# A linear-attention block: the output products of two chunks as seven products of halves

## The chip, the core and the metric

The kernel runs on one core of one Trainium2 chip. The time is the device time of one execution in microseconds (us); before the change it is 1804.88 us, the median of three runs (1803.95 to 1805.63).

The core has engines that each run their own queue of instructions in order and meet only at semaphores: TensorE (PE in the profile; PEld is its weight load), VectorE (DVE), ScalarE (ACT), GpSimd (POOL) and SyncE (SP), which here issues nearly all DMAs. Matrix products land in PSUM banks, the rest lies in SBUF.

## The reference, cut to what matters

x has shape 4 x 2048 x 512, all in float32.

```python
x = x + attention(layernorm(x))
x = x + ffn(layernorm(x))

# attention, with its own second norm of the normalized x, gain ln_g and offset ln_b:
qkv  = x_norm @ W_qkv + b_qkv                      # 512 -> 3 * 512
gate = sigmoid(x @ W_gate + b_gate); gate = gate / (mean(gate) + EPS)
q, k = relu(q * gate) ** 2 + EPS, relu(k * gate) ** 2 + EPS    # 16 heads of 32
out_t = (q_t . sum_{s<=t} k_s v_s) / (q_t . sum_{s<=t} k_s + EPS)
return out @ W_proj + b_proj                       # 512 -> 512: the "output product"

# ffn: 512 -> 128 -> 2048, gelu, 2048 -> 128 -> 512
```

## The kernel before, in words

The 8192 rows of x are 64 chunks of 128 tokens, 16 chunks to a sequence. After a start written out by hand for chunks 0 to 3, a loop over c = 4, 6, ..., 62 (line 1065) does one "double step" in each turn: gates, values, queries and keys of chunks c and c + 1; attention of chunk e = c - 1 and then of chunk c; and the feed-forward part of chunks c - 4 and c - 3. A tail finishes chunk 63 and the last feed-forward blocks.

Nothing is reordered by a scheduler: the program is built under a manual schedule (line 879), so each engine executes its instructions in the order of the Python calls. Tiles come from rings of buffers; a write into a buffer waits until the last reader of its former tile has finished. The rings that matter here are `tmp` (5 buffers of 128 x 512), `xn` (2, the normalized inputs), `xp` (12, the chunks of x), `oT` (1, the attention result with features first), `combos` (1) and the PSUM ring `bank` (6).

The gate/value and the query/key products are already done for two chunks at once by a scheme of seven half products (Strassen's, in Winograd's form): `combinations` (407) makes four sums and differences of the two chunks' features on GpSimd, `difference` (940) makes once four sums and differences of the quarters of the weights, and `half_product` (418) does two matmuls over half of the features. The output product is not: `project_out` (729) does four matmuls, 128 x 512 wide, for each chunk, and its `residual` adds the result to x and takes the mean and variance (`moments`, 221).

In one double step the calls in the loop give these orders:

- TensorE: gates and values of the pair (`ps_g`, `ps_gu`, ...), scores of e (`ps_a`), queries and keys (`ps_q` to `ps_k`), the feed-forward's first product (`ps_P`), weighted values of e (`ps_n`, `ps_m`, `ps_S`), four hidden products (`ps_h`, each followed two later by its `ps_Q`), the output product of e (`ps_p`), four more hidden products, scores of c, four more, weighted values of c, the last hidden products, the output product of c, and the two last feed-forward products (`ps_u`). Then the next turn begins with `ps_g`, whose second product `ps_gu` needs the second of the four combinations of chunks c + 2 and c + 3.
- GpSimd, from the output product of e on: the product of queries and running key sums of c (L598, it waits for VectorE's scan L588), the factors of the second layer norm (`second_norm`, L750 to L258: an inverse root by three Newton steps in small operations), the bias of the output product into x (L917), the bias of the feed-forward into two chunks of x (L760), the combinations for the next turn (L412 to L415) and one column of the next keys (L572), which the next scan on VectorE waits for.
- ScalarE, in the second half: the gelu of each hidden product (L797), the normalized inputs of the feed-forward (L264, they wait for `shift_f` of L258), more gelus, and the normalized chunks of a later pair.

The factors of the first norm (`first_norm_factors`, 335: 19 small GpSimd operations) are computed for four chunks at a time, inside `first_moments` ahead of the output product of e, and so in every other turn; in the turn c = 4 alone they stand behind `second_norm`. Input x is loaded at the head of turn c for chunks c + 6 and c + 7, into the buffers of c - 6 and c - 5. `pump(n)` issues the next n pieces of the feed-forward, of which there are 21 in a turn.

Of the kernel before, what the change touches and what calls it, by code (L numbers as in the profile page):

```python
# [60 lines left out]
def tile_linear_attention_block(  # L61
# [36 lines left out]
    of = out.flatten_outer_dims()  # L98

    const = ctx.enter_context(tc.tile_pool(name="const", bufs=1))  # L100
    xp = ctx.enter_context(tc.tile_pool(name="xp", bufs=12))
    work = ctx.enter_context(tc.tile_pool(name="work", bufs=1))
    psum = ctx.enter_context(tc.tile_pool(name="psum", bufs=1, space=bass.MemoryType.PSUM))

# [2 lines left out]
    def bank(name):  # L107
        return psum.tile([P, 512], F32, tag="bank", bufs=6, name=name)
# [38 lines left out]

    load_x(0)
    bg_one = row(b_gate, "a", 4, "bg_one", nc.scalar)
    bp_one = row(b_proj, "oT", 1, "bp_one", nc.scalar)  # L150
    b2_one = row(b2, "back", 1, "b2_one", nc.scalar)
    b_col = columns(ln_b, NK, "b_col", nc.scalar)
    g_col = columns(ln_g, NK, "g_col", nc.scalar)
# [23 lines left out]
    load_half(wqk, B22, w_qkv, 1, D)  # L177
    for c in range(NJ, 2 * NJ):
        load_x(c)
    wp = const.tile([P, NK, D], F32, tag="wp", name="wp")  # L180
    for g in range(NK):
        halves = w_proj[bass.ts(g, P), :].rearrange("(two p) n -> two p n", two=2)
        for half in range(2):
            at = (half ^ (g % 2)) * (P // 2)
            nc.sync.dma_start(wp[at : at + P // 2, g, :], halves[half])
    b1_col = columns(b1, NF, "b1_col", nc.sync)
    u1_sb, pieces = weights(u1, "u1_sb")
    load(pieces)
# [70 lines left out]
        return rs, shift  # L259

    def normalized(src, norm, j, name):
        t = work.tile([P, D], F32, tag="xn", bufs=2, name=name)
        rs, shift = norm
        nc.scalar.activation(  # L264
            t, src, AF.Identity, scale=rs[:, j : j + 1], bias=shift[:, j : j + 1]
        )
        return t
# [384 lines left out]
        return inv  # L652

    def numerators_over(c, num, inv):
        oT = work.tile([P, NK, P], F32, tag="oT", name=f"oT_{c}")
        for odd in range(2):
            by_parity = "p (two odd) t -> p two odd t"
            nc.vector.tensor_tensor(  # L658
                oT.rearrange(by_parity, odd=2)[:, :, odd],
                num[odd][:, 0 : 2 * P].rearrange("p (two t) -> p two t", t=P),  # L660
                inv.rearrange(by_parity, odd=2)[:, :, odd],
                ALU.mult,
            )
        return oT
# [62 lines left out]
        return oT  # L727

    def project_out(c, oT, mv):
        ps = bank(f"ps_p_{c}")  # L730
        for g in range(NK):
            nc.tensor.matmul(ps, oT[:, g, :], wp[:, g, :], start=(g == 0), stop=(g == NK - 1))  # L732

        def residual():

            xt = x_of[c]
            nc.vector.tensor_add(xt, ps, xt)  # L737
            moments(xt, mv, c % NJ)

        return residual  # L740


    x2T_of = {}
# [1 line left out]
    def second_norm(chunks, mv):  # L745

        at = slice(chunks[0] % NJ, chunks[-1] % NJ + 1)
        name = str(chunks[0])
        v = variances(len(chunks), f"f{name}")
        nc.gpsimd.tensor_scalar_add(v, mv[:, at, 1], EPS)  # L750
        rs = inverse_root_by_steps(v, "rs_f", name)
        norm = normalizer(mv[:, at, 0], rs, f"f{name}", nc.gpsimd)

        def normalize(n, c):
            b, j = divmod(c, NP)
            if b not in x2T_of:
                x2T_of[b] = work.tile([P, NP, NQ, NK, DH], F32, tag="x2T", name=f"x2T_{b}")
            xt = x_of[c]
            x2 = normalized(xt, norm, n, f"x2_{c}")
            nc.gpsimd.tensor_add(xt, xt, b2_row)  # L760
            to = x2T_of[b][:, j]
            if c < NC - 1:
                turned_in_quarters(x2, to, f"x2_{c}")
                return None

            return lambda: nc.scalar.copy(
                to.rearrange("p i k t -> p k i t"),
                features_first(x2, f"ps_x2_{c}").rearrange("p k (i t) -> p k i t", t=DH),
            )

        return [lambda n=n, c=c: normalize(n, c) for n, c in enumerate(chunks)]
# [112 lines left out]
    pairs = {}  # L884
    keys = {}
    combos = {}
    waiting = []

    def combine(c):
        combos[c] = combinations(c)  # L890

    def first_moments(n, factors=True):
        nonlocal mv_first
        if n >= NC:
            return
        if n % NJ == 0:
            mv_first = new_moments(f"mv_{n // NJ}")
        moments(x_of[n], mv_first, n % NJ)
        if n % NJ == NJ - 1 and factors:
            first_norm_factors(range(n + 1 - NJ, n + 1), mv_first)  # L900

    def new_keys_in_step(c):
        kT = new_keys(c)
# [14 lines left out]
        return inverse_denominators(e, keys[e][1])  # L918

    def rest_of_attention(e, scores, inv):  # L920
        return weighted(e, scores, pairs[e][1], pairs[e][0], values.pop(e), inv)

    def project_in_step(e, oT, put_off=False):
        nonlocal mv_second
        if e % NJ == 0:
            mv_second = new_moments(f"mv2_{e // NJ}")
        residual = project_out(e, oT, mv_second)
        if put_off:
            return residual
        residual()  # L930

    def nothing():
        pass

    def normalize_pair(c):
        if c < NC:
# [80 lines left out]
    keys[0] = kT, None  # L1017
    factors = sigmoids((2, 3), (g2, g3))
    values_of(2)
    for n in (8, 9):  # L1020
        load_x(n)
    held = {}

    def sums_of_first():
        sums_and_products(0)

    def scores_of_first():
        held["scores"] = scores_in_step(0)

    def features_and_keys():  # L1030
        for turn in turn_xl:
            turn()
        new_keys_in_step(1)

    second = queries_and_keys(
        2,
# [1 line left out]
        sums_of_first,  # L1038
        factors,
        scores_of_first,  # L1040
        features_and_keys,
    )
    inv = denominators_in_step(0)
    oT = rest_of_attention(0, held["scores"], inv)
    sums_and_products(1)
    scores = scores_in_step(1)
    combine(NJ)
    new_keys_in_step(2)
    inv = denominators_in_step(1)
    values_of(3)  # L1050
    project_in_step(0, oT)
    for to in (T1, T2, T4, T3):
        difference(wgv, to, nc.gpsimd)
    oT = rest_of_attention(1, scores, inv)
    sums_and_products(2)
    scores = scores_in_step(2)
    second()
    transfers_back()
    project_in_step(1, oT)
    inv = denominators_in_step(2)  # L1060
    waiting += second_norm([0, 1], mv_second)
    oT = rest_of_attention(2, scores, inv)


    for c in range(NJ, NC, 2):

        e = c - 1
        for n in (c + 6, c + 7):
            if n < NC:
                load_x(n)  # L1070
        held = {}

        def denominators():
            held["inv"] = denominators_in_step(e)

        later = c == NJ
        if later:
            gates_and_values(c, combos[c], lambda: new_keys_in_step(e))
            sums_and_products(e)
            while waiting:  # L1080
                waiting.pop(0)()
            transfers_back()
            residual = project_in_step(2, oT, put_off=True)
            turn_xl = normalize_pair(c + 2)
        else:
            gates_and_values(c, combos[c], denominators)
        scores = scores_in_step(e)

        def turn_features():
            for turn in turn_xl:  # L1090
                turn()

        if later:
            second = queries_and_keys(
                c, combos.pop(c), factors=residual, later=turn_features
            )
        else:
            second = queries_and_keys(c, combos.pop(c))

        rest += feed_forward((c - 4) // NP)  # L1100
        pump(1)
        if later:
            denominators()
        oT = rest_of_attention(e, scores, held["inv"])
        features_back()
        second()
        for n in range(c + 4 if later else c + 6, c + 8):
            first_moments(n, factors=not later)
        pump(4)
        project_in_step(e, oT)  # L1110
        transfers_back()
        pump(2)
        sums_and_products(c)
        waiting += second_norm([e - 1, e], mv_second)
        if later:
            first_norm_factors(range(c + 4, c + 8), mv_first)
        pump(2)


        scores = scores_in_step(c)  # L1120
        inv = denominators_in_step(c)
        pump(4)
        while waiting:
            waiting.pop(0)()
        transfers_back()
        oT = rest_of_attention(c, scores, inv)
        if c + 2 < NC:
            combine(c + 2)
        pump(6)
        project_in_step(c, oT)  # L1130
        if c + 2 < NC:
            pump(len(rest))
            sums_and_products(c + 1)
        for turn in normalize_pair(c + 4):
            turn()
# [4 lines left out]
    scores = scores_in_step(e)  # L1140
    pump(len(rest))
    sums_and_products(e)
    num = rest_of_attention(e, scores, None)
    waiting += second_norm([e - 1], mv_second)
    rest += feed_forward(NC // NP - 2)
    pump(1)
    inv = denominators_in_step(e)
    pump(3)
    oT = numerators_over(e, num, inv)
    waiting.pop(0)()  # L1150
    transfers_back()
    pump(2)
    project_in_step(e, oT)
    norm = second_norm([e], mv_second)
    pump(7)
    turn = norm[0]()
    pump(5)
    turn()
    pump(len(rest) - NP)
    last = feed_forward(NC // NP - 1)  # L1160
    last.pop(0)()
# [51 lines left out]
```

## Time and profile before

| what | value |
|---|---|
| median of three runs | 1804.88 us (1803.95 to 1805.63) |
| the profiled execution, its own time | 1804.6 us |
| its span on the core | 1802.8 us |
| mean granted TensorE clock | 0.998 of full speed |
| TensorE busy with matmuls | 1787.5 us (99%) |
| VectorE busy | 1248.5 us (69%) |
| GpSimd busy | 761.4 us (42%) |
| ScalarE busy | 659.8 us (37%) |
| DMA traffic | 174.21 MB, 97 GB/s on average |

A line of the page's groups reads: line of the code, engine, operation, output and inputs by the program's names, shape, count, then busy time and the mean length of one in ns, then the idle time of the engine ahead of them and what ended it. A line of the timeline reads: start, length, engine, line, operation; in brackets the idle time just before it and the engine that ended it. A float32 matrix product appears as two passes, so a chunk's output product of four matmuls is `x8`. Passes overlap in the pipeline, so their pace is read from start to start.

### The profile page before, as it was taken

What the parts mean: (1) busy time and instruction counts of PE and PEld (TensorE: products, weight loads), DVE (VectorE), ACT (ScalarE), POOL (GpSimd) and SP (SyncE); (2) the same over time, 40 slices, a digit from 0 to 9 for tenths busy, and PEclk for the clock granted to TensorE, in tenths of its full rate; (3) what the DMA queues carried; (4) which work ended last, traced back from release to release, by engine and by line L of the source; (5) the groups of instructions that cost most, each with busy time, mean ns of one, the idle gap of its engine ahead of it and who ended that gap; (6) DMA issues with size and microseconds to landing.
All of it is one profiled execution on the core that took longest, in us unless ns stands there. A gap on an engine that the chain in (4) does not pass through costs nothing.

```text
span 1802.8 us, 34139 instructions
## 1 busy us (share of the span) xinstructions
PE 1787.5 (99%) x12720; PEld 1059.6 (59%) x12720; DVE 1248.5 (69%) x2394; ACT 659.8 (37%) x1171; POOL 761.4 (42%) x1383
## 2 busy tenths in 40 slices
PE   9999999999999999999999999999999999999998
PEld 4455666555665556665556655566655566555666
DVE  7887766776767667676766676776767666766662
ACT  4333433333333334333333333343333334333333
POOL 3545454343544345442444534444334354343432
PEclk9999999999999999999999999999999999999999
DMA  7233332333323333223233232332332332322221
GB/s 228 77 101 93 112 100 89 93 89 101 113 83 93 98 90 112 97 92 91 89 103 107 86 93 90 101 112 92 93 92 90 105 104 87 92 79 90 91 71 47
DMA packets 286153, 174.21 MB, mean 97 GB/s; under 512 B 134558, under 2 KB 234910, under 8 KB 285860
## 3 DMA queue, kind: packets, MB, share of 16 engines
q1 hardware_dynamic: 284926, 172.03, 30.8%
q8 instruction: 100, 1.64, 0.4%
q14 instruction: 65, 0.53, 0.1%
q10 hardware_dynamic: 1062, 0.01, 0.0%
HBM read 89.94 MB, written 82.05 MB: 95 GB/s over the span
## 4 chain that ended last, share of the span: by engine, by line
PE 95%; DVE 2%; DMA 1%; POOL 1%; issue 1%; ACT 0%; SPq 0%; DVEq 0%; ACTq 0%; POOLq 0%
PE ps_h L795 13%; PE ps_Q L801 13%; PE ps_q L420 12%; PE ps_p L732 12%; PE ps_g L420 11%; PE ps_a L612 4%; PE ps_u L420 3%; PE ps_u L819 3%; PE ps_t L420 3%; PE ps_k L420 3%; PE ps_v L420 3%; PE ps_gt L420 3%; PE ps_gu L420 3%; PE ps_P L780 3%; PE ps_n L695 2%; PE ps_n L684 1%
## 5 line engine op out<-in xcount | busy, mean ns | idle before, releaser
L797 ACT ACTIVATE h<-ps_h,b_col 128x256 f32<-128x256 f32 x512 | 233.7, 470 | 292.4 <-PE ps_h L795 292.1
L795 PE MATMUL ps_h<-pT,v_sb 128*128 128x256 f32 x1024 | 303.6, 388 | 1.8 <-DVE pT L791 1.8
L801 PE MATMUL ps_Q<-h,u_sb 128*128 128x256 f32 x1024 | 298.5, 383 | 0.0
L732 PE MATMUL ps_p<-wp,oT 128*128 128x512 f32 x512 | 230.5, 593 | 0.4 <-DVE oT L658 0.4
L795 PEld LDWEIGHTS ps_h<-pT,v_sb 128*128 128x128 f32 x1024 | 187.0, 190 | 45.2 <-issue 15.3
L801 PEld LDWEIGHTS ps_Q<-h,u_sb 128*128 128x128 f32 x1024 | 189.1, 190 | 40.5 <-ACT h L797 17.4
L598 POOL TENSOR_TENSOR qsum<-qT,sums 128x512 f32<-128x512 f32 x64 | 75.4, 1178 | 322.3 <-DVE sums L588 318.2
L420 PE MATMUL ps_q<-wqk,xlT 128*128 128x512 f32 x372 | 177.9, 601 | 0.0
L737 DVE TENSOR_TENSOR x<-ps_p,x 128x512 f32<-128x512 f32 x64 | 44.2, 691 | 186.8 <-PE ps_p L732 186.8
L622 DVE TENSOR_TENSOR a<-ps_a,causal 128x512 f32<-128x512 f32 x256 | 158.3, 680 | 21.8 <-PE ps_a L612 21.8
L564 POOL TENSOR_SCALAR k<-k 128x512 f32<-128x512 f32 x64 | 95.8, 1496 | 170.9 <-DVE blocks_k L283 170.9
L420 PE MATMUL ps_g<-wgv,xlT 128*128 128x512 f32 x360 | 164.6, 593 | 0.1
L732 PEld LDWEIGHTS ps_p<-wp,oT 128*128 128x128 f32 x512 | 97.0, 190 | 97.0 <-issue 88.5
L517 POOL TENSOR_TENSOR u<-u,t 128x512 f32<-128x512 f32 x32 | 40.7, 1271 | 215.9 <-DVE t L515 215.9
L467 POOL TENSOR_TENSOR v<-gu,g 128x512 f32<-128x512 f32 x30 | 38.2, 1273 | 197.3 <-DVE g L462 197.3
L420 PEld LDWEIGHTS ps_g<-wgv,xlT 128*128 128x128 f32 x360 | 68.2, 190 | 86.2 <-issue 84.4
L420 PEld LDWEIGHTS ps_q<-wqk,xlT 128*128 128x128 f32 x372 | 68.1, 189 | 78.4 <-issue 52.9
L399 ACT ACTIVATE gate<-gate 128x512 f32<-128x512 f32 x64 | 40.3, 629 | 189.5 <-DVE gate L395 189.4
L488 ACT ACTIVATE t<-t,rg 128x512 f32<-128x512 f32 x32 | 23.1, 722 | 214.0 <-DVE t L486 214.0
L588 DVE TENSOR_TENSOR_SCAN sums<-keep,kT 128x516 f32<-128x516 f32 x64 | 79.3, 1240 | 28.9 <-ACT kT L577 19.5
L223 DVE BATCH_NORM_STATS2 st<-x 128x6 f32<-128x512 f32 x128 | 86.6, 677 | 8.9 <-DMA x<-in_L_attn_x_dram 6.7
L492 ACT ACTIVATE k<-u,rg 128x512 f32<-128x512 f32 x64 | 45.7, 714 | 118.4 <-DVE u L486 118.4
(175 smaller groups left out, 3213.8 us busy)
## 6 DMA issues: line engine op xcount, KB each, us to landing
x<-in_L_attn_x_dram SPq DMA_DIRECT2D x64, 256.0 KB
dr_q<-blocks_q SPq DMA_DIRECT2D x64, 256.0 KB
dr_k<-blocks_k SPq DMA_DIRECT2D x64, 256.0 KB
qT<-dr_q SPq DMA_DIRECT2D x256, 64.0 KB
kq<-dr_k SPq DMA_DIRECT2D x256, 64.0 KB
out_dram<-x SPq DMA_DIRECT2D x64, 256.0 KB
dr_x<-blocks_x SPq DMA_DIRECT2D x63, 256.0 KB
x2T<-dr_x SPq DMA_DIRECT2D x252, 64.0 KB
```

Source lines behind the costliest of these rows:

```text
L223: nc.vector.bn_stats(st, src)
L420: nc.tensor.matmul(ps, stationary[:, k, :], w[:, slot, k, :], start=(k == 0 and not more), stop=(k == NH - 1), skip_group_check=True,)
L564: nc.gpsimd.tensor_scalar_add(k, k, EPS)
L588: nc.vector.tensor_tensor_scan(sums.rearrange(flat), keep.rearrange(flat), kT.rearrange(flat), 0.0, ALU.mult, ALU.add,)
L598: nc.gpsimd.tensor_mul(qs.rearrange("p k (i t) -> p k i t", t=DH), qT.rearrange("p i k t -> p k i t"), sums[:, :, 1 : P + 1].rearrange("p ...
L612: nc.tensor.matmul(ps[r][:, bass.ts(g, P)], kT[rows, g, 1 : P + 1], qT[rows, :, g, :], start=True, stop=True,)
L622: nc.vector.tensor_tensor(a, ps[r].rearrange("p (g t) -> p g t", t=P), causal.unsqueeze(1).to_broadcast([P, NK, P]), ALU.mult,)
L732: nc.tensor.matmul(ps, oT[:, g, :], wp[:, g, :], start=(g == 0), stop=(g == NK - 1))
L780: nc.tensor.matmul(ps, u1_sb[:, k, :], x2T[:, :, :, k, :].rearrange("p j i t -> p (j i) t"), start=(k == 0), stop=(k == NK - 1),)
L795: nc.tensor.matmul(ps, v1_sb[:, 0, bass.ts(f, P)], held["p"], start=True, stop=True)
L797: nc.scalar.activation(h, ps, AF.Gelu_apprx_tanh, bias=b1_col[:, f : f + 1])
L801: nc.tensor.matmul(held["q"], u2_sb[:, f, :], held["h"].pop(f), start=(f == 0), stop=(f == NF - 1))
```

## The change

Chunks 0 and 1 keep a product each (`project_out`, now in two column halves because of the new layout of the weights). Every later pair e - 1, e is multiplied together by `project_two_out`: seven half products of two matmuls, 128 x 256 wide, in four half banks, with VectorE adding the pieces into the two chunks of x. `output_combinations` makes the four combinations of the two attention results on GpSimd, in the same ring `combos`. `wp` holds seven quarters and differences in place of the plain weight; it is loaded in 16 DMAs of half the width instead of 8, and its differences are made on GpSimd ahead of the loop.

With it go: `oT` has two buffers; the normalized inputs are drawn from `tmp`, and `xn` is gone; `xp` has 10 buffers, and x is loaded two chunks later; the first norm's factors are computed for two chunks in every turn up to c = 58, behind `second_norm`; the output product of c is gone from the second half of the turn, and the weighted values of c stand behind the last hidden product, just ahead of the two last feed-forward products; in the tail, chunks 62 and 63 are normalized together and both turned on TensorE.

```diff
-    xp = ctx.enter_context(tc.tile_pool(name="xp", bufs=12))
+    xp = ctx.enter_context(tc.tile_pool(name="xp", bufs=10))
...
-    wp = const.tile([P, NK, D], F32, tag="wp", name="wp")
+    wp = const.tile([P, 7, NH, D // 2], F32, tag="wp", name="wp")
...
-            nc.sync.dma_start(wp[at : at + P // 2, g, :], halves[half])
+            for col, slot in enumerate(((B11, B12), (B21, B22))[g // NH]):
+                nc.sync.dma_start(
+                    wp[at : at + P // 2, slot, g % NH, :], halves[half][:, bass.ts(col, D // 2)]
+                )
...
     def normalized(src, norm, j, name):
-        t = work.tile([P, D], F32, tag="xn", bufs=2, name=name)
+        t = temp(name)
...
+    def output_combinations(early, late, name):
+        s = work.tile([P, 4, NH, P], F32, tag="combos", name=f"outs_{name}")
+        lo, hi = slice(0, NH), slice(NH, NK)
+        nc.gpsimd.tensor_add(s[:, 0], early[:, lo], early[:, hi])
+        nc.gpsimd.tensor_sub(s[:, 1], s[:, 0], late[:, lo])
+        nc.gpsimd.tensor_sub(s[:, 2], late[:, lo], early[:, lo])
+        nc.gpsimd.tensor_sub(s[:, 3], late[:, hi], s[:, 1])
+        return s
...
+    def project_two_out(c, early, late, s, mv):
...
+        xe, xl = x_of[c], x_of[c + 1]
+        sums = temp(f"p_{c}")
+        u2, u3 = sums[:, left], sums[:, right]
+        t1 = temp(f"p1_{c}")[:, left]
...
+        ps5 = half_bank("pt")
+        half_product(ps5, s[:, 0], wp, T1)
+        nc.vector.tensor_add(xe[:, right], ps5, xe[:, right])
+        ps1 = half_bank("p")
+        half_product(ps1, late[:, lo], wp, B11)
+        nc.scalar.copy(t1, ps1)
+        ps6 = half_bank("pu")
+        half_product(ps6, s[:, 1], wp, T2)
+        nc.vector.tensor_add(u2, ps6, t1)
+        half_product(ps1, late[:, hi], wp, B21, more=True)
+        nc.vector.tensor_add(xl[:, left], ps1, xl[:, left])
+        ps7 = half_bank("pv")
+        half_product(ps7, s[:, 2], wp, T3)
+        nc.vector.tensor_add(u3, ps7, u2)
+        half_product(ps5, s[:, 3], wp, B22, more=True)
+        nc.vector.tensor_add(xl[:, right], xl[:, right], u2)
+        nc.vector.tensor_add(xl[:, right], ps5, xl[:, right])
+        half_product(ps7, early[:, hi], wp, T4, more=True)
+        moments(xl, mv, (c + 1) % NJ)
+        nc.vector.tensor_add(xe, xe, sums)
+        nc.vector.tensor_add(xe[:, left], ps7, xe[:, left])
+        moments(xe, mv, c % NJ)
...
-    def first_moments(n, factors=True):
+    def first_moments(n):
...
-        if n % NJ == NJ - 1 and factors:
-            first_norm_factors(range(n + 1 - NJ, n + 1), mv_first)
+        if n == 2 * NJ - 1:
+            first_norm_factors(range(NJ, 2 * NJ), mv_first)
...
-    for n in (8, 9):
-        load_x(n)
...
+    for to in (T1, T2, T4, T3):
+        difference(wp, to, nc.gpsimd)
...
     for c in range(NJ, NC, 2):
         e = c - 1
-        for n in (c + 6, c + 7):
+        for n in (c + 4, c + 5):
             if n < NC:
                 load_x(n)
...
-        oT = rest_of_attention(e, scores, held["inv"])
+        rest_of_attention(e, scores, held["inv"])
+        combine_results(e)
         features_back()
         second()
-        for n in range(c + 4 if later else c + 6, c + 8):
-            first_moments(n, factors=not later)
+        for n in (c + 4, c + 5):
+            first_moments(n)
         pump(4)
-        project_in_step(e, oT)
+        project_two_in_step(e)
         transfers_back()
         pump(2)
         sums_and_products(c)
         waiting += second_norm([e - 1, e], mv_second)
-        if later:
-            first_norm_factors(range(c + 4, c + 8), mv_first)
+        if c + 4 < NC:
+            first_norm_factors([c + 4, c + 5], mv_first)
         pump(2)
         scores = scores_in_step(c)
         inv = denominators_in_step(c)
         pump(4)
         while waiting:
             waiting.pop(0)()
         transfers_back()
-        oT = rest_of_attention(c, scores, inv)
         if c + 2 < NC:
             combine(c + 2)
-        pump(6)
-        project_in_step(c, oT)
+        pump(len(rest) - NP)
+        rest_of_attention(c, scores, inv)
         if c + 2 < NC:
             pump(len(rest))
             sums_and_products(c + 1)
```

In the start, the turn of chunks 4 and 5 into features-first form moves ahead of the scores of chunk 0, and `project_in_step(2)` is gone from the turn c = 4.

More of the change, by code (lines that the diff above doesn't have):

```diff
@@ L149, in tile_linear_attention_block @@
     bg_one = row(b_gate, "a", 4, "bg_one", nc.scalar)
-    bp_one = row(b_proj, "oT", 1, "bp_one", nc.scalar)
+    bp_one = row(b_proj, "oT", 2, "bp_one", nc.scalar)
     b2_one = row(b2, "back", 1, "b2_one", nc.scalar)
@@ L654, in numerators_over @@
     def numerators_over(c, num, inv):
-        oT = work.tile([P, NK, P], F32, tag="oT", name=f"oT_{c}")
+        oT = work.tile([P, NK, P], F32, tag="oT", bufs=2, name=f"oT_{c}")
         for odd in range(2):
@@ L730, in project_out @@
         ps = bank(f"ps_p_{c}")
[L731 to L740, printed above, removed]
+        for col, slots in enumerate(((B11, B21), (B12, B22))):
+            for g in range(NK):
+                nc.tensor.matmul(
+                    ps[:, bass.ts(col, D // 2)],
+                    oT[:, g, :],
+                    wp[:, slots[g // NH], g % NH, :],
+                    start=(g == 0),
+                    stop=(g == NK - 1),
+                    skip_group_check=True,
+                )
@@ new lines, in project_out @@
+        xt = x_of[c]
+        nc.vector.tensor_add(xt, ps, xt)
+        moments(xt, mv, c % NJ)
+    def output_combinations(early, late, name):
[6 more added lines that the diff above has]
+        return s
@@ new lines, in project_two_out, with half_bank @@
+    def project_two_out(c, early, late, s, mv):
+        lo, hi = slice(0, NH), slice(NH, NK)
+        left, right = slice(0, D // 2), slice(D // 2, D)
+        xe, xl = x_of[c], x_of[c + 1]
+        sums = temp(f"p_{c}")
+        u2, u3 = sums[:, left], sums[:, right]
+        t1 = temp(f"p1_{c}")[:, left]
+        def half_bank(name):
+            return bank(f"ps_{name}_{c}")[:, left]
+        ps5 = half_bank("pt")
[20 more added lines that the diff above has]
+        moments(xe, mv, c % NJ)
@@ L761, in normalize @@
             to = x2T_of[b][:, j]
-            if c < NC - 1:
+            if c < NC - 2:
                 turned_in_quarters(x2, to, f"x2_{c}")
@@ L886, in tile_linear_attention_block @@
     combos = {}
+    results = {}
     waiting = []
@@ L920, in rest_of_attention, with project_in_step @@
     def rest_of_attention(e, scores, inv):
-        return weighted(e, scores, pairs[e][1], pairs[e][0], values.pop(e), inv)
-    def project_in_step(e, oT, put_off=False):
+        results[e] = weighted(e, scores, pairs[e][1], pairs[e][0], values.pop(e), inv)
+    def project_in_step(e):
         nonlocal mv_second
@@ L926, in project_in_step, with combine_results, project_two_in_step @@
             mv_second = new_moments(f"mv2_{e // NJ}")
[L927 to L933, printed above, removed]
+        project_out(e, results.pop(e), mv_second)
+    def combine_results(e):
+        combos["out"] = output_combinations(results[e - 1], results[e], e - 1)
+    def project_two_in_step(e):
+        nonlocal mv_second
+        if (e - 1) % NJ == 0:
+            mv_second = new_moments(f"mv2_{e // NJ}")
+        project_two_out(
+            e - 1, results.pop(e - 1), results.pop(e), combos.pop("out"), mv_second
+        )
     def normalize_pair(c):
@@ L1027, in scores_of_first @@
     def scores_of_first():
-        held["scores"] = scores_in_step(0)
-    def features_and_keys():
         for turn in turn_xl:
             turn()
-        new_keys_in_step(1)
+        held["scores"] = scores_in_step(0)
     second = queries_and_keys(
@@ L1040, in tile_linear_attention_block @@
         scores_of_first,
-        features_and_keys,
+        lambda: new_keys_in_step(1),
     )
     inv = denominators_in_step(0)
-    oT = rest_of_attention(0, held["scores"], inv)
+    rest_of_attention(0, held["scores"], inv)
     sums_and_products(1)
@@ L1050, in tile_linear_attention_block @@
     values_of(3)
-    project_in_step(0, oT)
+    project_in_step(0)
     for to in (T1, T2, T4, T3):
         difference(wgv, to, nc.gpsimd)
-    oT = rest_of_attention(1, scores, inv)
+    rest_of_attention(1, scores, inv)
     sums_and_products(2)
@@ L1058, in tile_linear_attention_block @@
     transfers_back()
-    project_in_step(1, oT)
+    project_in_step(1)
+    for to in (T1, T2, T4, T3):
+        difference(wp, to, nc.gpsimd)
     inv = denominators_in_step(2)
     waiting += second_norm([0, 1], mv_second)
-    oT = rest_of_attention(2, scores, inv)
+    rest_of_attention(2, scores, inv)
     for c in range(NJ, NC, 2):
         e = c - 1
-        for n in (c + 6, c + 7):
+        for n in (c + 4, c + 5):
             if n < NC:
@@ L1082, in tile_linear_attention_block @@
             transfers_back()
-            residual = project_in_step(2, oT, put_off=True)
             turn_xl = normalize_pair(c + 2)
@@ L1091, in turn_features @@
                 turn()
-        if later:
[L1094 to L1098, printed above, removed]
+        second = queries_and_keys(c, combos.pop(c), queries=turn_features if later else None)
         rest += feed_forward((c - 4) // NP)
@@ L1114, in tile_linear_attention_block @@
         waiting += second_norm([e - 1, e], mv_second)
-        if later:
-            first_norm_factors(range(c + 4, c + 8), mv_first)
+        if c + 4 < NC:
+            first_norm_factors([c + 4, c + 5], mv_first)
         pump(2)
@@ L1142, in tile_linear_attention_block @@
     sums_and_products(e)
-    num = rest_of_attention(e, scores, None)
-    waiting += second_norm([e - 1], mv_second)
+    rest_of_attention(e, scores, None)
     rest += feed_forward(NC // NP - 2)
@@ L1148, in tile_linear_attention_block @@
     pump(3)
-    oT = numerators_over(e, num, inv)
-    waiting.pop(0)()
-    transfers_back()
+    results[e] = numerators_over(e, results[e], inv)
+    combine_results(e)
     pump(2)
[L1153 to L1158, printed above, removed]
+    project_two_in_step(e)
+    turn_x2 = second_norm([e - 1, e], mv_second)
+    pump(8)
+    turn_x2 = [turn() for turn in turn_x2]
+    pump(4)
+    for turn in turn_x2:
+        turn()
     pump(len(rest) - NP)
```

## The prediction

> **What bounds the kernel now.** I read the page's first part and chain first, then the group of the output product.
>
> ```profile
> span 1802.8 us, 34139 instructions
> PE 1787.5 (99%) x12720; PEld 1059.6 (59%) x12720; DVE 1248.5 (69%) x2394; ACT 659.8 (37%) x1171; POOL 761.4 (42%) x1383
> ...
> PE 95%; DVE 2%; DMA 1%; POOL 1%; issue 1%; ACT 0%; SPq 0%; DVEq 0%; ACTq 0%; POOLq 0%
> ...
> L732 PE MATMUL ps_p<-wp,oT 128*128 128x512 f32 x512 | 230.5, 593 | 0.4 <-DVE oT L658 0.4
> ```
>
> TensorE carries the chain from end to end and hardly ever waits: saved TensorE time is saved time, but so is every new TensorE wait lost time. The other engines are half idle on average; yet each runs its queue in order, so next comes where they stand against TensorE inside one double step. I take the one with c = 34 (timeline, 957 to 983 us), first TensorE (start, length, line):
>
> ```profile
> 957.76 3.60 PE L732 MATMUL ps_p<-wp,oT 128*128 128x512 f32 x8
> 961.19 0.59 PE L795 MATMUL ps_h<-pT,v_sb 128*128 128x256 f32 x2
> 961.62 0.59 PE L801 MATMUL ps_Q<-h,u_sb 128*128 128x256 f32 x2
> ...
> 979.29 1.88 PE L819 MATMUL ps_u<-v_sb,qs 128*128 128x512 f32 x4
> 981.00 1.88 PE L420 MATMUL ps_g<-wgv,xlT 128*128 128x512 f32 x4
> 982.72 1.88 PE L420 MATMUL ps_gu<-wgv,combos 128*128 128x512 f32 x4
> ```
>
> Starts give the true pace (lengths overlap): eight passes 512 wide take 961.19 - 957.76 = 3.43 us, 0.43 each; two passes 256 wide take 0.43 us, 0.215 each. Every f32 product is two passes. Call the end of the first product, 961.19, zero. The gate's second product (ps_gu), the first to need GpSimd's combinations, starts at +21.53. GpSimd and the VectorE row that releases it:
>
> ```profile
> 963.93 1.23 DVE L588 TENSOR_TENSOR_SCAN sums<-keep,kT 128x516 f32<-128x516 f32 x1 [0.90 <-ACT kT L577]
> ```
> ```profile
> 965.25 1.18 POOL L598 TENSOR_TENSOR qsum<-qT,sums 128x512 f32<-128x512 f32 x1 [6.71 <-DVE sums L588]
> 966.40 0.23 POOL L750 TENSOR_SCALAR v_f<-mv 128x2 f32<-128x2 f32 x1
> ...
> 970.59 0.22 POOL L258 TENSOR_SCALAR shift_f<-shift_f 128x2 f32<-128x2 f32 x1
> 970.77 1.28 POOL L917 TENSOR_TENSOR x<-x,bp_row 128x512 f32<-128x512 f32 x1
> 972.01 2.50 POOL L760 TENSOR_TENSOR x<-x,b_row 128x512 f32<-128x512 f32 x2
> ...
> 975.27 0.73 POOL L413 TENSOR_TENSOR combos<-combos,xlT 128x256 f32<-128x256 f32 x1
> ...
> 977.31 0.19 POOL L572 COPY kT<-sums 128x4 f32<-128x4 f32 x1
> ```
>
> From +4.06 to +16.3 GpSimd runs without a gap. L413, whose result ps_gu needs, ends at 976.00, +14.8: 6.7 us before TensorE asks. That margin is what the change spends.
>
> **The change, part by part.**
>
> *The product itself.* A pair of chunks took 16 passes of 0.43 = 6.88 us. Seven half products of two matmuls are 28 passes, 256 wide: 28 x 0.215 = 6.02 us, so 0.86 us saved a pair, 26.7 us over 31 pairs. (Chunks 0 and 1 alone: 16 passes of 0.215 for 8 of 0.43, nothing.) Against this stands a rule of the Trainium skill ("TensorE: Matmul & The Clock Gate", section "Back-to-back issue gap"): weight load and matmul set the spacing together, 81 ns at 128 columns and 131 ns at 512, so a narrow matmul is far from proportionally cheap. By a line between its two figures (an estimate) 256 columns cost 0.75 of 512: the pair would take 28 x 0.75 x 0.43 = 9.0 us, 66 us lost in all. The trace has L795 and L801 alternating, a new weight every pass, at exactly half: the 190 ns load fits inside 215. I take the row.
>
> *Added on VectorE:* six additions on halves from PSUM or SBUF (L658, 128x256: about 0.41), one half SBUF sum and one full one (0.69), for two full additions of 0.69: about +2.2 us a pair. Most lies between the products. After the last product's end it has: 0.4 (xl right; its product ended 0.86 earlier), moments 0.83, sum 0.7, 0.4, moments 0.83, ending at about +2.5. The scan L588 waits for ScalarE's kT until +2.74 anyway, so this is hidden with 0.25 us left; without that cover each microsecond goes straight into the chain below. The half product that reuses ps7's bank waits for u3, which ends about 0.2 us ahead of it.
>
> *Added on GpSimd:* four combinations of 0.73 (as L412 to L415), queued between L529 and the second L564, where GpSimd idles (its next piece is qsum, 6.7 us idle before): no cost. They reuse the single combos buffer, free since ps_k. The ScalarE copy of half a bank (row L436, 0.59 for a full one) has one product, 0.86 us, to finish in: no wait. wp's differences are 4 x 1.27 us once on GpSimd; twice as many wp DMAs are 8 x 0.78 us (L185: 6.21 us for eight) on SP's queue, moving the last weight issue to about 40 us, where SP next has work at 39.67; u, v and the features behind it are not late. Both at nothing.
>
> *Loads.* x is loaded for c+4, c+5 into 10 buffers, not c+6, c+7 into 12: each load waits for the same chunk's output (c-6), and its moments stay the same distance behind. Normalized inputs among the five temporaries: counting 15 allocations a double step, each finds a predecessor five back already read. No cost. Ahead of the loop, turning chunks 4 and 5 (eight TensorE transposes, L273, 1.0 us) moves ahead of chunk 0's scores, and `combine(c + 2)` ahead of the weighted products: each keeps its place in GpSimd's and SP's queues, and its price.
>
> *The first norm's factors.* Here it costs. They were 19 small GpSimd operations once in two double steps, in an idle stretch ahead of qsum. They now come in every double step and stand behind the second norm's factors, ahead of bp, b2 and the next combinations. Their size per call does not matter (0.28 us apiece at 128x2, x4 and x8). The double step c = 4 of this very trace has that order:
>
> ```profile
> 143.13 0.23 POOL L258 TENSOR_SCALAR shift_f<-shift_f 128x2 f32<-128x2 f32 x1
> 143.44 0.23 POOL L346 TENSOR_SCALAR v<-mv 128x4 f32<-128x4 f32 x1
> ...
> 148.62 1.27 POOL L917 TENSOR_TENSOR x<-x,bp_row 128x512 f32<-128x512 f32 x1
> ```
>
> L917 starts 5.49 us after L258, in the step above 0.18 us: +5.3 us. L413 now ends at 14.8 + 5.3 = +20.1. And TensorE comes earlier, because the second output product (3.43 us) is gone from this stretch: ps_gu at 21.53 - 3.43 = +18.1. It waits 2.0 us, and a restart costs up to 0.3 (ps_h after a wait for pT: six passes in 1.54 us, not 1.29): about +20.3.
>
> *Behind it.* GpSimd's kT column (L572) ends at +16.3 + 5.3 = +21.6; the scan waits for it, then both blocks_xl, L440 and L444 (3.8 us in that c = 4 step) end near +25.4. The product that overwrites ps_g needs L444 and would start at 20.3 + 5.15 = 25.45: another 0.2 us.
>
> *The weighted products, moved behind the hidden layer:* they stood between the waits of ScalarE and the last hidden products and covered this:
>
> ```profile
> 969.23 0.47 ACT L797 ACTIVATE h<-ps_h,b_col 128x256 f32<-128x256 f32 x1 [0.39 <-PE ps_h L795]
> 970.84 1.52 ACT L264 ACTIVATE x<-x,shift_f,rs_f 128x512 f32<-128x512 f32 x2 [1.14 <-POOL shift_f L258]
> 972.27 0.45 ACT L797 ACTIVATE h<-ps_h,b_col 128x256 f32<-128x256 f32 x1
> ```
>
> h number 12 is done at 972.72, +11.5; TensorE without the cover wants it at +10.35: 1.3 us of wait. In most steps this lies inside the 2.0 us above (TensorE reaches ps_gu at 19.4, still early). Alone it would be 1.3 - 0.86 = +0.45 a step.
>
> *Sum.* A double step: -0.86 + 2.2 + 0.2 = about +1.5 us. The 28 steps c = 4 to 58 call the factors: +42. Three of them begin a sequence and have 0.6 us less weighted work to cover: +1.5. Steps 60 and 62 have only the ScalarE wait: +0.9. At the start project 2 goes (-3.4), but VectorE's scan and score masks (L588 at 105.9 to L498 at 112.4) hold TensorE to nearly the old time; at the end the pair costs 6.02 for 3.43, with a second chunk normalized and turned on TensorE, about +3.5. Total about +48 on the profiled 1804.6 us (span 1802.8), which is the median 1804.88 of the runs: 1851 rounded.
>
> **Rivals.** *The same mechanism, half as large:* GpSimd's chain starts or runs about 1 us earlier against TensorE than I line it up; then the ScalarE wait remains: 30 x 0.45 plus 3.5 = 1822. For it: the alignment rests on few steps. Against: they repeat to 0.1 us. *Faster:* the forecast turns if L413 ends by +18.6 instead of +20.1 and h 12 comes within 0.5 us of need, that is, if GpSimd's 5.3 us are mostly overlapped; then the product's gain stays, 1804.9 - 26.7 = 1778, or down to -10 with half a wait: 1795. For it: GpSimd is idle 58%. Against: its order is fixed and the chain has no gap in it. *Slower still:* the 0.25 us of VectorE's cover is missed by about 1 us (the additions at 0.7 us instead of 0.4), which lengthens the chain one for one: 28 more, 1879. The narrow-matmul rule would give 1804.9 + 66, plus waits, more.
>
> **How the numbers follow.** Main case 0.74 (1836 to 1864), half-size 0.10 (1810 to 1836), slower still 0.09, faster 0.07. The range 1818 to 1866 takes in the main case and most of the half-size one. A change of 0.2% (3.6 us) is about what a measurement can tell; nearly nothing falls inside it.
>
> **What would show it.** TensorE: 28 passes at 0.215; ps_gu waiting about 2 us for L413's successor, some 28 times; VectorE's scan waiting for the kT column; a ps_Q wait for h behind L264; TensorE busy near 97% or less. Wrong if the qsum no longer starts near +4.1, if ps_gu does not wait, or if 256-wide passes of wp exceed 0.22 us.

## The result, and the profile after

The changed kernel takes 1856.9 us (median of four runs, 1854.8 to 1858.6) against 1805.3 us before (a median of four here, the three runs told above among them): a ratio of 1.029 (95% interval 1.027 to 1.030). The forecast was 1851 us, slower. The profiled execution took 1857.51 us, 52.9 more than that of before, and so did its span. First the page's opening part and its chain:

```profile
span 1855.7 us, 35857 instructions
PE 1787.7 (96%) x13112; PEld 1128.1 (61%) x13112; DVE 1321.7 (71%) x2579; ACT 665.9 (36%) x1203; POOL 907.2 (49%) x1761
...
PE 61%; POOL 22%; DVE 10%; issue 6%; ACT 1%; DMA 0%; SPq 0%; DVEq 0%; POOLq 0%; ACTq 0%
```

TensorE's busy time did not fall at all, though 25.4 us of passes went (31 pairs, each 2 x 3.43 us before and 6.04 us now). Busy time swallows a part of every stall: the row behind a wait is longer (0.70 for 0.59), and the row ahead counts as busy its 0.16 us of overhang, the part of its length beyond its pace (0.59 for 0.43). So busy time is the wrong place to look for a loss. The chain tells more: GpSimd holds 22% of it where it held 1%. The list of TensorE's waits (us in total, times, longest) names the two that recur:

```profile
PE ps_Q L853 <- ACT h L849: 31.8, 30, 1.1
PE ps_gu L423 <- POOL combos L416: 15.9, 28, 1.1
...
PE ps_P L832 <- DMA out_dram<-x: 2.0, 1, 2.0
```

Thirty waits for h (the ScalarE wait of the forecast) and 28 for the combinations (its GpSimd wait). The same double step, c = 34, on TensorE (start, length, line); the output product of the pair ends at 988.46, which is zero again:

```profile
982.42 1.03 PE L423 MATMUL ps_pt<-wp,outs 128*128 128x256 f32 x4
...
1000.05 0.70 PE L853 MATMUL ps_Q<-h,u_sb 128*128 128x256 f32 x2 [1.06 <-ACT h L849]
...
1006.17 1.88 PE L423 MATMUL ps_g<-wgv,xlT 128*128 128x512 f32 x4
1008.56 1.98 PE L423 MATMUL ps_gu<-wgv,combos 128*128 128x512 f32 x4 [0.51 <-POOL combos L416]
...
1039.18 1.03 PE L423 MATMUL ps_pt<-wp,outs 128*128 128x256 f32 x4
```

And GpSimd in that step:

```profile
992.52 1.19 POOL L601 TENSOR_TENSOR qsum<-qT,sums 128x512 f32<-128x512 f32 x1 [8.59 <-DVE sums L591]
...
997.86 0.22 POOL L261 TENSOR_SCALAR shift_f<-shift_f 128x2 f32<-128x2 f32 x1
...
1003.28 1.29 POOL L970 TENSOR_TENSOR x<-x,bp_row 128x512 f32<-128x512 f32 x1
...
1007.78 0.73 POOL L416 TENSOR_TENSOR combos<-combos,xlT 128x256 f32<-128x256 f32 x1
...
1009.81 0.20 POOL L575 COPY kT<-sums 128x4 f32<-128x4 f32 x1
```

qsum starts at +4.06, as before. From the start of L261 to the start of the bp addition 5.42 us now pass, taken up by the first norm's factors (0.18 us before); L416 ends at +20.05 and the kT column at +21.55. ps_gu starts at +20.10, the moment L416 is done. A whole step, from one ps_pt to the next, takes 56.76 us (982.42 to 1039.18) where it took 55.29 (the first product of that step before, from 957.76 to 1013.05).

Where the 52.9 us lie, by the times of the same instructions in both traces: 2.3 up to ps_P of c = 4, in the first double step; 42.4 in the 29 steps from there to ps_P of c = 62; 8.2 behind that.

### The profile page after: what moved, and what is told of

It is laid out like the page before. It is cut to its first block, busy times and chain, and to the rows that moved or that the text cites. A ratio compares the mean times of both kernels' runs of the same rounds, so it can differ in the third digit from the quotient of the medians.

```text
span 1855.7 us, 35857 instructions
## 1 busy us (share of the span) xinstructions
PE 1787.7 (96%) x13112; PEld 1128.1 (61%) x13112; DVE 1321.7 (71%) x2579; ACT 665.9 (36%) x1203; POOL 907.2 (49%) x1761
## 4 chain that ended last, share of the span: by engine, by line
PE 61%; POOL 22%; DVE 10%; issue 6%; ACT 1%; DMA 0%; SPq 0%; DVEq 0%; POOLq 0%; ACTq 0%
PE ps_q L423 11%; PE ps_g L423 8%; PE ps_h L847 4%; POOL x L812 4%; PE ps_gu L423 3%; PE ps_p L423 3%; PE ps_t L423 3%; PE ps_k L423 3%; PE ps_pt L423 3%; PE ps_Q L853 3%; PE ps_P L832 3%; PE ps_v L423 3%; PE ps_gt L423 3%; PE ps_u L423 3%; DVE st L226 2%
## 5 line engine op out<-in xcount | busy, mean ns | idle before, releaser
L849 ACT ACTIVATE h<-ps_h,b_col 128x256 f32<-128x256 f32 x512 | 227.6, 468 | 304.7 <-PE ps_h L847 304.4
L853 PE MATMUL ps_Q<-h,u_sb 128*128 128x256 f32 x1024 | 302.5, 387 | 31.8 <-ACT h L849 31.8
L847 PEld LDWEIGHTS ps_h<-pT,v_sb 128*128 128x128 f32 x1024 | 190.8, 191 | 32.6 <-DVE pT L843 2.8
L423 PE MATMUL ps_g<-wgv,xlT 128*128 128x512 f32 x360 | 170.0, 601 | 0.9 <-DVE gu L447 0.9
L615 PEld LDWEIGHTS ps_a<-qT,kT 32*128 32x128 f32 x2048 | 63.3, 186 | 33.4 <-issue 21.2
L970 POOL TENSOR_TENSOR x<-x,bp_row 128x512 f32<-128x512 f32 x64 | 82.2, 1284 | 0.0
L812 POOL TENSOR_TENSOR x<-x,b_row 128x512 f32<-128x512 f32 x64 | 79.9, 1272 | 0.9 <-ACT x L267 0.9
```

The costliest lines, as they stand in the source:

```text
L423: nc.tensor.matmul(ps, stationary[:, k, :], w[:, slot, k, :], start=(k == 0 and not more), stop=(k == NH - 1), skip_group_check=True,)
L615: nc.tensor.matmul(ps[r][:, bass.ts(g, P)], kT[rows, g, 1 : P + 1], qT[rows, :, g, :], start=True, stop=True,)
L847: nc.tensor.matmul(ps, v1_sb[:, 0, bass.ts(f, P)], held["p"], start=True, stop=True)
L849: nc.scalar.activation(h, ps, AF.Gelu_apprx_tanh, bias=b1_col[:, f : f + 1])
L853: nc.tensor.matmul(held["q"], u2_sb[:, f, :], held["h"].pop(f), start=(f == 0), stop=(f == NF - 1))
L970: nc.gpsimd.tensor_add(x_of[e], x_of[e], bp_row)
```

## The experiments

The theory going in: a double step saves 0.86 us on TensorE, but the factors in front of GpSimd's combinations make ps_gu late, and a ScalarE wait ahead of it, uncovered by the weighted products that moved, hides inside that lateness. The chief rival: the seven half products, with their VectorE additions, cost what they save or more. A second: the ScalarE wait is the whole loss.

**The factors early.**

```diff
         for n in (c + 4, c + 5):
             first_moments(n)
+        if c + 4 < NC:
+            first_norm_factors([c + 4, c + 5], mv_first)
         pump(4)
         project_two_in_step(e)
...
         waiting += second_norm([e - 1, e], mv_second)
-        if c + 4 < NC:
-            first_norm_factors([c + 4, c + 5], mv_first)
```

> The changed kernel, with the first norm's factors of chunks c+4 and c+5 issued right behind their moments, in GpSimd's idle stretch ahead of qsum, where the kernel before had them. Theory (the factors stand in GpSimd's queue ahead of the combinations that ps_gu needs; behind that wait hides a ScalarE wait of the hidden layer): ps_gu no longer waits, ps_Q still waits about 1.1 to 1.3 us a double step, so 1828 to 1832 us. Rival 1 (the seven half products and their VectorE additions are what costs the time): unchanged, 1857. Rival 2 (only the ScalarE wait of ps_Q costs, and the ps_gu wait is what is left of it): unchanged, about 1857.

Measured: 1830.5 us, ratio to before 1.014 (1.013 to 1.016). TensorE's waits, first line:

```profile
PE ps_Q L853 <- ACT h L849: 35.7, 30, 2.7
```

ps_gu is gone from the list, and the 30 waits for h remain. Both rivals said 1857. The factors' place was worth 26 us of the loss. L416 ends about 4.6 us ahead of ps_gu here, in the same step.

**The weighted products back.**

```diff
         transfers_back()
+        rest_of_attention(c, scores, inv)
         if c + 2 < NC:
             combine(c + 2)
         pump(len(rest) - NP)
-        rest_of_attention(c, scores, inv)
```

> The changed kernel, with the weighted products of c put back ahead of the next combinations and the rest of the hidden layer, as the kernel before had them. Theory: the ps_Q waits of 1.1 us go, but TensorE then waits as much longer for the combinations at ps_gu (about 2 us a double step instead of 1.1), so about 1855, within 3 us of the changed kernel. Rival 1 (the seven products cost it): 1857. Rival 2 (only the ScalarE wait costs): the whole 30 x 1.1 to 1.3 us come back, about 1818 to 1822.

Measured: 1854.9 us, ratio 1.028 (1.026 to 1.029), within 2.1 us of the changed kernel.

```profile
PE ps_gu L423 <- POOL combos L416: 28.8, 28, 1.6
PE ps_u L871 <- DVE qs L866: 15.5, 30, 0.5
```

The waits for h (31.8 us in all) are gone and the time is still there. The waits of ps_gu take up a part of it: they grew from 15.9 to 28.8 us, 1.0 us a step where about 2 were expected. The rest is in the second line, which was not foreseen: 30 waits of ps_u, half a microsecond each, for VectorE's copy of ps_Q. The second rival (1818 to 1822) falls; the first, with its 1857, is too near the theory's 1855 for this run to tell them apart.

**Both.** The two edits together.

> The changed kernel with both edits of the two runs before it: the factors early, the weighted products back in their place. Theory: both covers are restored, the double step takes 0.86 us less than in the kernel before, and only the start (about 2 us) and the end (about 8 us) still lose: 1788 to 1793 us, faster than the kernel before. Rival 1 (the seven products cost it): about 1857. Rival 2: about 1820, with the ps_gu wait unchanged.

Measured: 1812.7 us, ratio 1.004 (1.002 to 1.005): the expectation missed by 20 us, and neither rival as stated (1857; about 1820 with the ps_gu wait unchanged) was met. This is the miss that taught most. The waits for the combinations and the recurring ones for h are gone, and what heads the list are 30 waits of ps_u for qs, 15.5 us in all. On TensorE in that step:

```profile
978.57 1.49 PE L853 MATMUL ps_Q<-h,u_sb 128*128 128x256 f32 x6
980.58 1.98 PE L871 MATMUL ps_u<-v_sb,qs 128*128 128x512 f32 x4 [0.52 <-DVE qs L866]
982.40 1.88 PE L423 MATMUL ps_g<-wgv,xlT 128*128 128x512 f32 x4
```

Six passes of 0.215 end at 979.86; ps_u starts at 980.58, 0.72 later, and takes 1.82 to the next start where 1.72 is its price: 0.82 us lost in a step, just what the halves save (2 x 3.43 less 6.04; the step takes 55.25 us). In the kernel before, the output product of c stood between the last ps_Q and ps_u, and covered VectorE's copy. The change took that cover away and put the weighted products in its place, which took them from in front of h. There were two covers for two waits; now there is one. At this point the first rival was alive again in a milder form: 55.25 could also be the price of the seven products, if they give back just what they save.

**The kernel before, with the factors as the changed kernel has them.**

```diff
-            first_moments(n, factors=not later)
+            first_moments(n, factors=False)
...
         if later:
             first_norm_factors(range(c + 4, c + 8), mv_first)
+        elif c + 6 < NC:
+            first_norm_factors([c + 6, c + 7], mv_first)
```

(One more buffer for unscale and one fewer for sd, to make room.)

> The kernel before, with the first norm's factors of the next two chunks issued in every double step behind the second norm's, as the changed kernel has them, instead of four chunks at once in every other double step. Theory: GpSimd ends the combinations at about +20.1 us, and TensorE, which still has the second output product in that stretch, asks at +21.5: hidden, 1805 to 1807 us. Rival (19 more GpSimd operations in that stretch cost by themselves, by delaying VectorE's scan or holding up other engines): up to 1.5 us a double step, about 1847.

Measured: 1805.3 us, ratio 1.000 (0.999 to 1.001). Its product ends at 962.23 in that step, GpSimd's L413 and TensorE's ps_gu stand so:

```profile
981.47 0.73 POOL L413 TENSOR_TENSOR combos<-combos,xlT 128x256 f32<-128x256 f32 x1
```
```profile
983.77 1.88 PE L420 MATMUL ps_gu<-wgv,combos 128*128 128x512 f32 x4
```

L413 ends at +19.97, as late as in the changed kernel, and costs nothing, since ps_gu comes at +21.54. So the same five microseconds of GpSimd work are free in front of the second output product and cost about a microsecond a step without it (the 1830.5 of early factors against 1856.9, over 28 steps: 0.94).

**The normalization behind the hidden layer.** From the run with early factors; here the weighted products stay in front of ps_u, and ScalarE's second normalizations (1.5 us, at which h waited) are issued after the hidden layer's last piece.

```diff
-        pump(4)
+        pump(len(rest) - NP)
         while waiting:
             waiting.pop(0)()
         transfers_back()
         if c + 2 < NC:
             combine(c + 2)
-        pump(len(rest) - NP)
         rest_of_attention(c, scores, inv)
```

> The changed kernel with the factors early, the weighted products left where the change put them (ahead of the last products ps_u), and the second norm's two ScalarE normalizations issued behind all of the hidden layer instead of between its pieces. Theory after the run with both edits (the weighted products can cover one of two waits: that of ps_Q for h, or that of ps_u for VectorE's copy of ps_Q; the second output product covered the other before): neither wait is left, a double step takes 55.3 - 0.9 = 54.4 us, and the time is the 1830.5 of the factors alone less 30 x 1.3 = 1791 us (1788 to 1795). Rival (the seven products themselves give back what they save, so no order of the work gets below 55.2 us a double step): 1812, as with both edits.

Measured: 1796.1 us, ratio 0.995 (0.994 to 0.996): faster than the kernel before.

```profile
946.24 1.03 PE L423 MATMUL ps_pt<-wp,outs 128*128 128x256 f32 x4
...
1000.71 1.03 PE L423 MATMUL ps_pt<-wp,outs 128*128 128x256 f32 x4
```

A double step takes 54.47 us (946.24 to 1000.71), as the theory said; the rival's 55.2 falls, and with it the idea that the seven products give back their gain. The total missed the expected 1791 by 5 us, and the waits say where:

```profile
PE ps_P L832 <- DMA out_dram<-x: 8.9, 1, 8.9
```

No recurring wait is left, but the one at the end grew from 2.0 to 8.9 us. (The profile names the transfer after out_dram; what ps_P reads is x2T, the turned chunks 60 and 61, and the wait is gone in the next run, which turns them on TensorE.) The later normalization sends the DMA that turns these chunks later too, and in the last double step its product is the next thing TensorE needs. Counted from the step's ps_pt, the normalizations start 2.2 us later than in the changed kernel and the x2T transfers are issued 5.0 us later; where the other 2.8 come from is not shown.

**The tail turned on TensorE.**

```diff
-            if c < NC - 2:
+            if c < NC - 4:
                 turned_in_quarters(x2, to, f"x2_{c}")
...
+        turn_late = []
         while waiting:
-            waiting.pop(0)()
+            turn_late.append(waiting.pop(0)())
...
         rest_of_attention(c, scores, inv)
+        for turn in turn_late:
+            if turn is not None:
+                turn()
```

> The kernel of the run beside this one, with chunks 60 and 61 turned on TensorE in the last double step, as 62 and 63 are, instead of by DMA. Theory: the 2.0 to 2.8 us wait of ps_P for that DMA goes, and with it the granted clock of 0.5 for about 5 us behind it; 16 transposes (about 2 us) are added: 2 to 4 us less than the run beside it. Rival (the drop of the clock comes from the light work ahead of it and not from that wait): the wait goes but the clock still drops, and the time stays within 1 us.

Measured: 1787.7 us, ratio to before 0.990 (0.989 to 0.991), 8.4 less than the run beside it. Expected were 2 to 4, reckoned on a wait of 2.0 to 2.8 us; the wait that was there to remove was 8.9, and the added transposes took 1.1 us where about 2 were expected. Stretches of 4 us behind this point (from:to, length, busy time of PE, PEld, DVE, ACT, POOL, then the granted clock, DMA share, GB/s) in the run beside it:

```profile
1738.00:1742.00 4.00, 0.00 (x0) 0.00 (x0) 0.00 (x0) 0.00 (x0) 0.00 (x0) 0.50 0.52 182
1742.00:1746.00 4.00, 3.50 (x8) 2.52 (x8) 0.00 (x0) 0.00 (x0) 0.00 (x0) 0.50 0.02 6
1746.00:1750.00 4.00, 3.48 (x9) 2.61 (x9) 3.51 (x9) 1.15 (x3) 0.00 (x0) 0.50 0.02 4
```

and in this one:

```profile
1738.00:1742.00 4.00, 3.48 (x17) 2.63 (x16) 3.04 (x6) 1.34 (x3) 3.08 (x3) 1.00 0.30 110
1742.00:1746.00 4.00, 4.00 (x20) 3.53 (x19) 2.34 (x7) 1.32 (x3) 1.85 (x3) 1.00 0.00 0
```

The wait and the half clock behind it are both gone. The rival (the clock falls for the light work ahead) is not borne out. This version is 1% faster than the kernel before: the seven products with all three waits covered.

## Why the prediction was right, step by step

*The product:* right. 28 passes, seven rows of four, start 0.86 to 0.87 us apart, 6.04 us in all; two products took 2 x 3.43 us, so 0.82 us are saved (forecast 0.86). The rule of the Trainium skill that spoke against it ("TensorE: Matmul & The Clock Gate", "Back-to-back issue gap"), by which I estimated 9.0 us, does not hold for these passes; row L795 did.

*VectorE's additions hidden behind kT:* right with nothing to spare. They were to end at +2.5 with 0.25 us in hand. VectorE now goes from its last moments straight into the scan, without a wait:

```profile
991.04 0.18 DVE L227 BATCH_NORM_AGGREGATE mv<-st 128x2 f32<-128x6 f32 x1
991.21 1.23 DVE L591 TENSOR_TENSOR_SCAN sums<-keep,kT 128x516 f32<-128x516 f32 x1
```

The scan starts at +2.75 (before: +2.74), but VectorE ends its work there, not 0.25 earlier. The row of sizes 0.41 was right; the gaps between dependent operations took the rest. The "slower still" rival was that close.

*Four combinations, the copy, wp's differences and DMAs, the loads at nothing:* right for the loop, taken together. With all three waits covered, the step falls from 55.29 to 54.47 us, by the 0.82 us that the products save, which leaves nothing for them. They were not tried one by one.

*The factors:* right. L416 ends at +20.05 (forecast +20.1), ps_gu starts at +20.10 (forecast +20.3), kT ends at +21.55 (forecast +21.6). Early factors remove the wait, and the kernel before bears the same work for nothing, which is what the step claimed: it is not the work that costs but the cover that left.

*The further 0.2 us behind it:* right. The product that overwrites ps_g runs 3.62 us for 3.43.

*The ScalarE wait inside the 2.0:* right. ps_Q loses 1.06 us idle and about 0.25 of overhang and restart (forecast 1.3), ps_gu the remaining 0.77, together 2.1; with the 0.2 behind it, less 0.86, the step gains 1.4 to 1.5, and 1.47 is measured. Without the ps_gu wait, in the run with early factors, the step takes 55.87 us, 0.58 more than before (forecast +0.45).

*The loop's sum:* 44.4 forecast for 30 steps, 44.0 for the first 29 of them; these took 42.4. The forecast's last addition has a slip: +48 on the 1804.6 us that it names makes 1853, and 1851 is +48 on the span.

*The ends of the program:* here the forecast was short. The start was put at zero and took 2.3 us. The lines of the changed kernel, then those of the kernel before, and the stretches from 112 us in the same order:

```profile
113.38 3.53 PE L423 MATMUL ps_q<-wqk,xlT 128*128 128x512 f32 x4 [2.60 <-DVE t L501]
116.74 1.88 PE L423 MATMUL ps_t<-wqk,combos 128*128 128x512 f32 x4
```
```profile
112.76 1.88 PE L420 MATMUL ps_q<-wqk,xlT 128*128 128x512 f32 x4
114.48 1.88 PE L420 MATMUL ps_t<-wqk,combos 128*128 128x512 f32 x4
```
```profile
112.00:116.00 4.00, 2.62 (x3) 1.18 (x4) 2.01 (x4) 0.00 (x0) 1.81 (x2) 0.64 0.18 53
```
```profile
112.00:116.00 4.00, 4.00 (x11) 1.80 (x10) 3.33 (x7) 0.00 (x0) 0.00 (x0) 1.00 0.15 45
```

VectorE's scan and masks do hold TensorE to nearly the old time, as forecast: the first of these products starts 0.6 us later than before, after a wait of 2.6 us. (A wait of 1.5 us for features at 61 us, behind the transposes that moved, was not forecast either; by here at most those 0.6 us are left of it.) But the four passes then take 3.36 us instead of 1.72, at a granted clock of 0.64 instead of 1.00, and these 1.6 us no term of the forecast held. The end was put at +3.5 and took 8.2. Its term lacked two things: the 2.0 us wait of ps_P for the DMA of chunks 60 and 61, which TensorE reaches sooner because the output product of c = 62 is gone from in front of it, and what the clock did then:

```profile
1804.00:1808.00 4.00, 2.77 (x9) 1.93 (x10) 0.86 (x2) 0.00 (x0) 3.07 (x3) 0.77 0.15 55
1808.00:1812.00 4.00, 4.00 (x10) 3.16 (x10) 3.10 (x9) 1.42 (x3) 0.55 (x1) 0.50 0.01 4
1812.00:1816.00 4.00, 4.00 (x18) 3.42 (x17) 0.42 (x1) 1.23 (x3) 1.54 (x3) 0.88 0.00 0
```

The ten passes from 1808 to 1812 take twice their time. By the product of clock deficit and time in these three lines, 0.23 x 4 + 0.50 x 4 + 0.12 x 4 = 3.4 us; a part of the first lies in a wait, so about 3. So what the forecast lacked at both ends is the clock behind a wait, and at the end the wait as well.

*What none of the steps said:* that the output product of c, too, was a cover, for VectorE's copy of ps_Q. In the changed kernel the weighted products stand there, so the number did not suffer; but the "faster" rival, which asked only for early combinations and a timely h, would have been wrong about an easy repair: putting the weighted products back, with the factors early, gives 1812.7, not 1778.

## What to carry to other kernels

When an edit shortens the bounding engine's work, list for each removed or moved stretch which results of other engines matured behind it, and price every one; here a gain of 0.82 us a step became a loss of 1.47 because two stretches of TensorE work (the second output product and the weighted products) had covered three waits (ps_gu, ps_Q, ps_u), and one of the two was removed; only covering all three brought the gain in. A wait that appears may hide a second one, and that a third: undo the causes in pairs, not only one by one, and look at the waits' list of each run. Look separately at the last turn of the loop, where nothing stands behind a late transfer.

## What was not expected of the hardware

How little idleness halves the clock. Waits of 1.06 and 0.5 us in every double step leave the granted clock at 1.00 for the whole loop, and so does a single one of 1.34 us near the end of the last run (1.00 from 1730 to 1734 us). One wait of 2.0 us at the end of the changed kernel, with 0.5 us more three microseconds on, cost 3.4 us by the product above, which is 6.8 us at 0.5. The wait of 2.6 us at its start cost 1.7 by the same product (0.64 and 0.93 in the two stretches from 112 to 120 us). The Trainium skill ("TensorE: Matmul & The Clock Gate", "HAM oscillation — how this bites in real kernels") gives as its abstract rule no gaps over about 3.4 us; these are shorter, and the measurement decides. With the same 2.0 us wait in the run with early factors the stretches from 1775 to 1783 had 0.82 and 0.76 (by the product above 1.7 us, not 3.4), so the price varies; what sets it within these waits stays open. With the wait of 8.9 us, which ended at 1742.5, the clock stood at 0.50 from 1742 to 1750 us, while TensorE was busy for 7.0 of the 8.
